# Two 64-token products on four 64x64 tiles, and a chunk's output projection half a slot behind its transposes

## The chip, the cores and the metric

The kernel runs on one core of a Trainium2 chip. The metric is the device time of one execution in microseconds; the time before is the median of three runs. The profile is of one further execution. Engines: PE is TensorE (matrix products; PEld are its weight loads), DVE is VectorE, ACT is ScalarE, POOL is GpSimd, and SP is SyncE, which here issues DMAs and nothing else. An engine's instructions run in the order of its own queue.

## The reference, cut to what matters

Two layers over 2 sequences of 1024 tokens with 256 features. The first adds a gated delta-rule attention and a mixture of low-rank experts to the input; the second adds a gated linear attention and a 2:4-sparse feed-forward unit. All numbers are float32. The change is in the first layer's attention only: 16 key heads and 32 value heads of 128 channels, two value heads to a key head.

```python
q, k, v = silu(causal_conv4(xn @ W_qkvz))       # q, k normalised per head, q * 128**-0.5
beta = sigmoid(b); g = -exp(A_log) * softplus(a + dt_bias)
def step(S, inp):                               # per sequence and head; S is 128 x 128
    qt, kt, vt, gt, bt = inp
    S = S * exp(gt)
    delta = (vt - kt @ S) * bt
    S = S + outer(kt, delta)
    return S, qt @ S
core = scan(step, 0, over the 1024 tokens)
gated = rmsnorm(core * silu(z)) * norm_w
out = gated @ W_out                             # (32*128) -> 256
```

## The kernel before

**Chunks.** The scan is computed in chunks of 64 tokens per sequence. A tile's 128 partitions hold 64 tokens of sequence 0 (partitions 0 to 63, `LO`) and the same 64 of sequence 1 (64 to 127, `HI`). Value heads go in 8 groups of four (`HPG`), which belong to two key heads (`KPG`); head n of a group belongs to key head m = n // 2. A group has 16 chunks; two neighbouring chunks are a pair, so there are 64 pairs and 128 chunks.

**One chunk.** With N the masked and decayed key products of a chunk, the update of a whole chunk needs the inverse of a 64x64 triangular matrix per sequence and head. The functions, in a pair's order:

- `pair_scores`: the decays `lb` are exponentiated (L508 to L512), q-k and k-k products are made (`kq`, L520), and DVE multiplies the two into `np` (L526): `np[:, 0]` is N, `np[:, 1]` the masked query products. SP then sends N to `nat` (four DMAs, L530) and to a DRAM buffer `natd` (two, L536), and brings its 8x8 diagonal blocks back as `n` (eight, L540).
- `pair_lanes`: DVE inverts the 8x8 blocks (L558 to L582); the result `E` goes through DRAM (L584, L586) into `U`.
- `pair_inverse`: PE and DVE join 8x8 inverses to 32x32 and 64x64 ones (`px`, `pyt`, `L`, `xs`). The result `invT` is 128x128 per head and chunk, block diagonal over the two sequences.
- `chunk_tokens`: keys and values are transposed to tokens on partitions; POOL scales the keys into `ktok` (L688), ACT the values into `vtok` (L697).
- `chunk_state`: PE makes `pks` and `pqs` from the state `S` (L716); DVE corrects `vtok` (L719), POOL decays `S` (L724); PE makes `pf` = inverse times values (L734), ACT copies it to `f` (L736); PE makes the state's increment `pS` from `ktok` and `f` (L743) and the output part `po` from `np[:, 1]` and `f` (L747); DVE adds `pS` to `S` (L754) and `po` to `qs` (L758) and gates with `z` (L760); ACT sums squares (L765).
- `chunk_output`: POOL makes the norm (L775 to L782); PE transposes (`yT`), ACT copies to `yTs` (L788), PE multiplies with `wo` (L792), DVE adds to the residual (L794).

`pf` multiplies whole 128x128 matrices, four per chunk. `pS` runs on four 64x64 tiles of the PE array (two row halves by two column halves), `po` on two (rows of a sequence to the same partitions of the output).

**Slots.** The layer runs in slots, one per pair. In a slot, generators of different pairs are interleaved step by step: each has a window of the slot (`add(kind, lo, hi, ...)`), and the one whose next step is due first goes. So a slot holds the scores of pair p, the inverse of pair p-1, the state of both chunks of pair p-2, the output of that pair's first chunk, and the output of pair p-3's second chunk, beside four blocks of the convolution (`conv_block`, L363) and two gates `z` for coming pairs. This gives the priority in which instructions are put on the engines' queues; an instruction whose inputs are expected later can be put behind others.

**PSUM.** All of PSUM is one pool of eight banks (`ps_tile`) for the whole program.

## Time and profile before

| What | us |
|---|---|
| median of three runs | 2953.18 |
| their range | 2949.0 to 2954.69 |
| profiled execution, its own time | 2948.61 |
| its span from first to last instruction | 2946.9 |
| PE busy in the span | 2647.8 |
| DVE, ACT, POOL busy | 1914.8, 1716.6, 1516.5 |
| granted PE clock, mean share | 0.971 |

How to read the lines that follow. The page gives each engine's busy time and its share of the span, then the span in 40 slices with the busy share in tenths. The chain of waits is followed back from the last instruction: at each step to what released it, or to the instruction before it on its engine. A line of the windows gives a stretch, its length and the busy time and instruction count of PE, PEld, DVE, ACT and POOL, then the granted clock, the DMA engines' busy share and GB/s. A line of waits names who waited for whom, the total, the count and the longest. A group has the line, engine, operation, output and inputs, shapes and count; then busy time, mean ns of one, and the engine's idle time before it with what ended it. A line of the chain in order of time has the start, the length, and the engine with what it writes and its line, or a DMA.

### The profile page before, as it was taken

How to read it: one execution, taken by the hardware profiler on the slowest of the kernel's cores; microseconds unless marked ns; L12 is line 12 of the kernel's file. 1: busy time of each engine (PE TensorE's matmuls, PEld its weight loads, DVE VectorE, ACT ScalarE, POOL GpSimd, SP SyncE). 2: the span in 40 equal slices, each digit the busy share in tenths (PEclk: the TensorE clock that was granted, in tenths of full speed). 3: DMA queues.
4: the chain of work that ended last, by engine and by line, in shares of the span. 5: the costliest groups of instructions: out<-in, count | busy, mean ns of one | idle time of the engine just before them, and what ended most of it. 6: DMA issues, size and time to landing. Idle time of an engine off the chain costs nothing.

```text
span 2946.9 us, 87779 instructions
## 1 busy us (share of the span) xinstructions
PE 2647.8 (90%) x36502; PEld 1680.6 (57%) x36502; DVE 1914.8 (65%) x3845; ACT 1716.6 (58%) x4121; POOL 1516.5 (51%) x2690
## 2 busy tenths in 40 slices
PE   6998689998999899989999999999989998989997
PEld 2444356665666566655655666566655665654565
DVE  7652666676677666767767666677676677645544
ACT  4432566675666666666666667666666666544321
POOL 2222456666666666666666666666665666630000
PEclk9998899999999999999999999999999999999999
DMA  3001111111111111111111111111111111110000
GB/s 77 4 1 57 37 28 35 36 43 28 35 35 43 28 35 35 44 28 43 34 38 28 42 35 35 28 42 36 36 27 35 28 37 20 29 57 3 1 15 15
DMA packets 265965, 95.22 MB, mean 32 GB/s; under 512 B 220512, under 2 KB 244192, under 8 KB 265568
## 3 DMA queue, kind: packets, MB, share of 16 engines
q1 hardware_dynamic: 261872, 86.67, 13.2%
q8 instruction: 287, 4.70, 0.7%
q10 hardware_dynamic: 3696, 2.95, 0.4%
q14 instruction: 110, 0.90, 0.1%
HBM read 53.63 MB, written 27.53 MB: 28 GB/s over the span
## 4 chain that ended last, share of the span: by engine, by line
PE 32%; DVE 22%; ACT 13%; POOL 12%; issue 7%; DMA 7%; SPq 6%; DVEq 0%; POOLq 0%; ACTq 0%
DVE conv L363 6%; PE pj L152 5%; SPq L540 3%; PE out L792 3%; ACT gsq L765 3%; DMA n<-natd 3%; DVE qs L758 2%; DMA natd<-np 2%; DVE S L754 2%; POOL S L724 2%; DVE z L760 2%; PE y L1074 2%; POOL rn L447 2%; PE pg L152 2%; SPq L530 2%
## 5 line engine op out<-in xcount | busy, mean ns | idle before, releaser
L363 DVE SCALAR_TENSOR_TENSOR conv<-raw,convw,conv 128x512 f32<-128x512 f32 x768 | 644.3, 841 | 188.6 <-ACT conv L358 184.2
L152 PE MATMUL pj<-xnT,w 128*128 128x512 f32 x1024 | 509.4, 622 | 8.5 <-DMA w<-in_W_qkvz 8.5
L792 PE MATMUL out<-wo,yTs 128*128 128x256 f32 x1024 | 284.1, 425 | 106.7 <-ACT yTs L788 106.7
L719 DVE SCALAR_TENSOR_TENSOR vtok<-pks,neG,vtok 128x128 f32<-128x128 f32 x480 | 144.8, 342 | 251.7 <-PE pks L716 247.4
L765 ACT ACTIVATE gsq<-z 128x128 f32<-128x128 f32 x512 | 157.7, 308 | 246.3 <-DVE z L760 240.9
L152 PEld LDWEIGHTS pj<-xnT,w 128*128 128x128 f32 x1024 | 188.8, 197 | 187.0 <-issue 182.1
L792 PEld LDWEIGHTS out<-wo,yTs 128*128 128x128 f32 x1024 | 200.6, 206 | 143.0 <-ACT yTs L788 113.4
L724 POOL TENSOR_TENSOR S<-S,eEnd 128x512 f32<-128x512 f32 x224 | 257.7, 1170 | 26.7 <-PE pqs L716 26.3
L152 PE MATMUL z<-wz,xnT 128*128 128x512 f32 x512 | 240.4, 593 | 0.0
L356 ACT COPY raw<-pj 128x512 f32<-128x512 f32 x256 | 147.5, 576 | 144.3 <-PE pj L152 95.5
L754 DVE TENSOR_TENSOR S<-S,pS 128x512 f32<-128x512 f32 x224 | 148.5, 684 | 123.8 <-POOL S L724 110.8
L734 PE MATMUL pf<-vtok,invT 128*128 128x128 f32 x1024 | 167.1, 289 | 31.4 <-DVE vtok L719 31.2
L347 POOL COPY raw<-tails 128x6 f32<-128x6 f32 x192 | 68.8, 359 | 239.4 <-DVE conv L363 189.7
L358 ACT ACTIVATE conv<-pj,convw 128x512 f32<-128x512 f32 x256 | 176.9, 691 | 0.0
L729 ACT ACTIVATE qs<-pqs,neG 128x128 f32<-128x128 f32 x480 | 136.3, 365 | 56.9 <-PE pqs L716 54.9
L372 ACT ACTIVATE kq<-conv 128x512 f32<-128x512 f32 x128 | 81.3, 635 | 144.3 <-DVE conv L363 141.4
L734 PEld LDWEIGHTS pf<-vtok,invT 128*128 128x128 f32 x1024 | 135.9, 190 | 50.8 <-DVE vtok L719 43.2
L782 POOL TENSOR_TENSOR z<-z,rms 128x512 f32<-128x512 f32 x128 | 145.5, 1136 | 10.1 <-POOL rms L779 0.2
L688 POOL TENSOR_TENSOR ktok<-kt,wend 128x512 f32<-128x512 f32 x120 | 145.6, 1213 | 7.5 <-ACT kt L684 7.5
L360 POOL COPY tails<-raw 128x6 f32<-128x6 f32 x192 | 60.7, 316 | 156.5 <-ACT raw L356 156.5
L743 PE MATMUL pS<-f,ktok 64*64 64x128 f32 x3840 | 132.5, 275 | 7.6 <-ACT f L736 7.5
L603 PE MATMUL px<-L,natm 32*32 32x32 f32 x8192 | 101.7, 198 | 40.8 <-DVE L L645 22.7
(323 smaller groups left out, 5885.0 us busy)
## 6 DMA issues: line engine op xcount, KB each, us to landing
lb<-grows SPq DMA_DIRECT2D x128, 128.0 KB
natd<-np SPq DMA_DIRECT2D x128, 128.0 KB
w<-in_W_qkvz SPq DMA_DIRECT2D x16, 512.0 KB
nat<-np SPq DMA_DIRECT2D x256, 32.0 KB
n<-natd SPq DMA_DIRECT2D x512, 4.0 KB
ed<-E SPq DMA_DIRECT2D x64, 128.0 KB
U<-ed SPq DMA_DIRECT2D x64, 128.0 KB
wz<-in_W_qkvz SPq DMA_DIRECT2D x16, 256.0 KB
```

The costliest lines, as they stand in the source:

```text
L152: k.nc.tensor.matmul(ps, lhsT_of(kt), rhs_of(kt), start=(kt == 0), stop=(kt == KT - 1))
L356: nc.scalar.copy(chunks(raw[:, :, KSIZE - 1 :]), pv)
L358: nc.scalar.activation(chunks(y), pv, AF.Copy, scale=tap(KSIZE - 1))
L363: k.anchor = nc.vector.scalar_tensor_tensor(y, shifted, tap(j), y, ALU.mult, ALU.add).ins
L688: nc.gpsimd.tensor_tensor(pair(x.k), bcast(kt, 2, 2), bcast(wend, 3, P), ALU.mult)
L719: nc.vector.scalar_tensor_tensor(x.v[:, i, :], pks[:, i, :], at(k.neG, i), x.v[:, i, :], ALU.mult, ALU.add)
L724: nc.gpsimd.tensor_tensor(k.S[:, b], k.S[:, b], bcast(k.eEnd[:, b, t, h.h0 : h.h0 + HPG], 2, P), ALU.mult)
L734: nc.tensor.matmul(pf[:, i, :], invT[:, i, :], x.v[:, i, :], start=True, stop=True)
L754: nc.vector.tensor_tensor(k.S[:, b], k.S[:, b], pS[b], ALU.add)
L765: nc.scalar.activation(sq, x.z[:, i, :], AF.Square, accum_out=x.sumsq[:, i : i + 1])
L782: nc.gpsimd.tensor_tensor(y, y, bcast(rms, 2, P), ALU.mult)
L792: nc.tensor.matmul(po[:, 0:D], yT[:, i, :], wo[:, i, :], start=(i == 0), stop=(i == HPG - 1))
```

## The change

In `chunk_state`, `pf` becomes eight 64x64 products per chunk. For the value heads of the first key head, a sequence's rows go to the same half of the output's partitions; for those of the second they go to the other half (`across`). So `pf` uses all four tiles, and f, the keys' `ktok`, the query products `np[:, 1]` and the state `S` hold the two sequences swapped for heads 2 and 3. `po` crosses back and also uses all four. The order of heads in both is 0, 2, 1, 3. Both products share a new PSUM tile `fo` of two banks, one per key head, in a pool of its own with one buffer; the shared pool keeps six banks in this layer.

To swap heads 2 and 3, DVE and POOL write that half to a side tile (`npo`, `ktoko`), and two DMAs on SP's queue move it across the partitions. `invT` is kept without its zero blocks. `eEnd`, the decay of a chunk, is swapped when it is made.

The last part of `chunk_output` becomes `chunk_project` and gets windows of its own: the first chunk's projection runs in the slot after its transposes, the second chunk's in the later half of the slot.

```diff
 def pair_scores(k, pools, pr):
-    for s in range(2):
-        by = kq[:, :, :, s].rearrange("p x m i -> p (x m) i")
-        nc.vector.tensor_tensor(pairs(pr.np[:, s]), pairs(lb), bcast(by, 2, 2), ALU.mult)
-        if s == 0:
-            yield
+    by = kq[:, :, :, 0].rearrange("p x m i -> p (x m) i")
+    nc.vector.tensor_tensor(pairs(pr.np[:, 0]), pairs(lb), bcast(by, 2, 2), ALU.mult)
+    yield
+    other = wk.tile([P, PC, 2, CT], F32, tag="npo", name=f"npo{pr.name}", bufs=1)
+    for m, out in enumerate((pr.np[:, 1, :, 0:2], other)):
+        two = slice(2 * m, 2 * m + 2)
+        nc.vector.tensor_tensor(out, lb[:, :, two], bcast(kq[:, :, m, 1], 2, 2), ALU.mult)
+    for rows, across in ((LO, HI), (HI, LO)):
+        nc.sync.dma_start(pr.np[across, 1, :, 2:4], other[rows])
     for n, r in enumerate(QUARTERS):
         nc.sync.dma_start(pr.nat[r], pr.np[r, 0, :, :, QUARTERS[n % 2]])
...
 def chunk_tokens(k, pools, x):
-        nc.gpsimd.tensor_tensor(pair(x.k), bcast(kt, 2, 2), bcast(wend, 3, P), ALU.mult)
+        other = wk.tile([P, 2, P], F32, tag="ktoko", name=f"ktoko{x.name}")
+        for m, out in ((1, other), (0, x.k[:, 0:2])):
+            wend = h.wend[:, c, 2 * m : 2 * m + 2]
+            nc.gpsimd.tensor_tensor(out, bcast(kt[:, m], 1, 2), bcast(wend, 2, P), ALU.mult)
+        for rows, across in ((LO, HI), (HI, LO)):
+            nc.sync.dma_start(x.k[across, 2:4], other[rows])
...
 def chunk_state(k, pools, x):
-                    nc.tensor.matmul(out[rows, two, :], q, k.S[:, b, two, :], start=True, stop=True)
+                    nc.tensor.matmul(out[rows, two, :], q, k.S[:, b ^ m, two, :], start=True, stop=True)
...
-    pf = four(k, f"pf{x.name}")
-    for i in range(HPG):
-        nc.tensor.matmul(pf[:, i, :], invT[:, i, :], x.v[:, i, :], start=True, stop=True)
+    fo = k.psum2.tile([P, KPG, 2, 2, P], F32, tag="fo", name=f"fo{x.name}")
+    pf, po = fo[:, :, 0], fo[:, :, 1]
+    across = lambda r, m: halves[r ^ m][1]
+    for i in range(2):
+        for m in range(KPG):
+            for r, rows in halves:
+                n = 2 * m + i
+                nc.tensor.matmul(pf[across(r, m), m, i, :], invT[rows, n, :], x.v[rows, n, :], start=True, stop=True)
...
-    po = four(k, f"po{x.name}")
-    for i in range(HPG):
-        for b, rows in halves:
-            nc.tensor.matmul(po[rows, i, :], x.pair.np[rows, 1, x.at, i, :], f[rows, i, :], start=True, stop=True)
+    for i in range(2):
+        for m in range(KPG):
+            for r, rows in halves:
+                n = 2 * m + i
+                nc.tensor.matmul(
+                    po[across(r, m), m, i, :], x.pair.np[rows, 1, x.at, n, :], f[rows, n, :], start=True, stop=True
+                )
...
 def chunk_output(k, pools, x):
-    yT = pools.work.tile([P, HPG, P], F32, tag="yT", name=f"yTs{x.name}")
-    nc.scalar.copy(yT, pt)
+    x.yT = pools.work.tile([P, HPG, P], F32, tag="yT", name=f"yTs{x.name}")
+    nc.scalar.copy(x.yT, pt)
     yield
+
+def chunk_project(k, pools, x):
+    nc, sm, h, c = k.nc, pools.small, x.h, x.c
+    wo = group_weights(k, pools, "o", h.grp)
     po = ps_tile(k, f"out{x.name}")
...
 def delta_layer(k, I):
-                add("output1", 0.05, 0.5, chunk_output(k, pools, pair(p - 3).chunks[1]))
+                one, two = pair(p - 3).chunks
+                add("output1", 0.05, 0.5, chunk_output(k, pools, two))
+                add("project0", 0.05, 0.4, chunk_project(k, pools, one))
+                add("project1", 0.55, 0.9, chunk_project(k, pools, two), "output1")
...
 def two_layers(ctx, tc, I, out):
-        delta_layer(k, I)
+        early.close()
+        with psum("psum1", 6) as k.psum, psum("psum2", 1) as k.psum2:
+            delta_layer(k, I)
```

Outside the layer the program has its eight banks as before, in pools of their own.

More of the change, by code (lines that the diff above doesn't have):

```diff
@@ L249, in delta_gates @@
         nc.tensor.matmul(ps, k.ones[rows], flat(g)[rows], start=True, stop=True)
-        nc.scalar.activation(flat(k.eEnd[:, b]), ps, AF.Exp)
+        by_key = lambda a: a.rearrange("p (t g m j) -> p t g m j", t=NTILE, g=NGROUP, m=KPG)
+        for m in range(KPG):
+            mine = by_key(flat(k.eEnd[:, b ^ m]))[:, :, :, m]
+            nc.scalar.activation(mine, by_key(ps)[:, :, :, m], AF.Exp)
         yield
@@ L653, in pair_inverse @@
     for n, r in enumerate(QUARTERS):
-        (nc.gpsimd.tensor_copy, nc.scalar.copy)[n % 2](invT[r, :, r], U[r])
+        (nc.gpsimd.tensor_copy, nc.scalar.copy)[n % 2](invT[r, :, QUARTERS[n % 2]], U[r])
     yield
@@ L670, in pair_inverse @@
     for q, copy in ((0, nc.scalar.copy), (2, nc.vector.tensor_copy)):
-        copy(invT[QUARTERS[q], :, QUARTERS[q + 1]], pyt[QUARTERS[q]])
+        copy(invT[QUARTERS[q], :, QUARTERS[1]], pyt[QUARTERS[q]])
     yield
@@ L685, in chunk_tokens @@
         x.k = wk.tile([P, HPG, P], F32, tag="ktok", name=f"ktok{x.name}")
-        pair = lambda a: a.rearrange("p (m i) c -> p m i c", m=KPG)
-        wend = h.wend[:, c, :].rearrange("p (m i) -> p m i", m=KPG)
-        nc.gpsimd.tensor_tensor(pair(x.k), bcast(kt, 2, 2), bcast(wend, 3, P), ALU.mult)
+        other = wk.tile([P, 2, P], F32, tag="ktoko", name=f"ktoko{x.name}")
[4 more added lines that the diff above has]
+            nc.sync.dma_start(x.k[across, 2:4], other[rows])
         yield
@@ L730, in chunk_state @@
         yield
-    pf = four(k, f"pf{x.name}")
-    for i in range(HPG):
-        nc.tensor.matmul(pf[:, i, :], invT[:, i, :], x.v[:, i, :], start=True, stop=True)
+    fo = k.psum2.tile([P, KPG, 2, 2, P], F32, tag="fo", name=f"fo{x.name}")
[6 more added lines that the diff above has]
+                nc.tensor.matmul(pf[across(r, m), m, i, :], invT[rows, n, :], x.v[rows, n, :], start=True, stop=True)
     f = wk.tile([P, HPG, P], F32, tag="f", name=f"f{x.name}")
-    nc.scalar.copy(f, pf)
+    by_key = lambda a: a.rearrange("p (m i) d -> p m (i d)", m=KPG)
+    flat = lambda a: a.rearrange("p m i d -> p m (i d)")
+    nc.scalar.copy(by_key(f), flat(pf))
     yield
     if not x.last:
-        pS = [four(k, f"pS{x.name}_{b}") for b in range(NB)]
+        pS = [four(k, f"pS{x.name}_{r}") for r in range(NB)]
         for i in range(HPG):
-            for b, rows in halves:
+            for r, rows in halves:
                 for cols in (LO, HI):
-                    nc.tensor.matmul(pS[b][cols, i, :], x.k[rows, i, cols], f[rows, i, :], start=True, stop=True)
-    po = four(k, f"po{x.name}")
-    for i in range(HPG):
-        for b, rows in halves:
-            nc.tensor.matmul(po[rows, i, :], x.pair.np[rows, 1, x.at, i, :], f[rows, i, :], start=True, stop=True)
+                    nc.tensor.matmul(pS[r][cols, i, :], x.k[rows, i, cols], f[rows, i, :], start=True, stop=True)
+    for i in range(2):
+        for m in range(KPG):
+            for r, rows in halves:
+                n = 2 * m + i
+                nc.tensor.matmul(
+                    po[across(r, m), m, i, :], x.pair.np[rows, 1, x.at, n, :], f[rows, n, :], start=True, stop=True
+                )
     yield
@@ L755, in chunk_state @@
     yield
-    no = po
+    no = flat(po)
     if not x.first:
-        nc.vector.tensor_tensor(qs, qs, po, ALU.add)
-        no = qs
-    nc.vector.tensor_tensor(x.z, no, x.z, ALU.mult)
+        nc.vector.tensor_tensor(by_key(qs), by_key(qs), no, ALU.add)
+        no = by_key(qs)
+    nc.vector.tensor_tensor(by_key(x.z), no, by_key(x.z), ALU.mult)
     yield
@@ L771, in chunk_output @@
     nc, sm, h, c = k.nc, pools.small, x.h, x.c
-    wo = group_weights(k, pools, "o", h.grp)
+    group_weights(k, pools, "o", h.grp)
     pair = lambda a: a.rearrange("p (m i) -> p m i", m=KPG)
@@ L786, in chunk_output @@
         nc.tensor.transpose(pt[:, i, :], y[:, i, :], k.ident)
-    yT = pools.work.tile([P, HPG, P], F32, tag="yT", name=f"yTs{x.name}")
-    nc.scalar.copy(yT, pt)
+    x.yT = pools.work.tile([P, HPG, P], F32, tag="yT", name=f"yTs{x.name}")
+    nc.scalar.copy(x.yT, pt)
     yield
+def chunk_project(k, pools, x):
+    nc, sm, h, c = k.nc, pools.small, x.h, x.c
+    wo = group_weights(k, pools, "o", h.grp)
     po = ps_tile(k, f"out{x.name}")
     for i in range(HPG):
-        nc.tensor.matmul(po[:, 0:D], yT[:, i, :], wo[:, i, :], start=(i == 0), stop=(i == HPG - 1))
+        nc.tensor.matmul(po[:, 0:D], x.yT[:, i, :], wo[:, i, :], start=(i == 0), stop=(i == HPG - 1))
     res = k.res[:, h.t0 + c, :]
@@ L849, in delta_layer @@
         k.tails = const.tile([P, 4 * KPG, NB, KSIZE - 1], F32, tag="tails", name="tails")
-        k.invT = [const.tile([P, PC, HPG, P], F32, tag=f"invT{i}", name=f"invT{i}") for i in range(2)]
+        k.invT = [const.tile([P, PC, HPG, CT], F32, tag=f"invT{i}", name=f"invT{i}") for i in range(2)]
         k.S = const.tile([P, NB, HPG, P], F32, tag="S", name="S")
@@ L1353, in two_layers @@
     k.keep = ctx.enter_context(tc.tile_pool(name="keep", bufs=1))
-    k.psum = ctx.enter_context(tc.tile_pool(name="psum", bufs=8, space=bass.MemoryType.PSUM))
+    psum = lambda name, bufs: tc.tile_pool(name=name, bufs=bufs, space=bass.MemoryType.PSUM)
     k.res = k.keep.tile([P, NTILE, D], F32, tag="res", name="res")
@@ L1364, in two_layers @@
     k.xnT = k.keep.tile([P, KT, N], F32, tag="xnT", name="xnT")
+    early = ctx.enter_context(ExitStack())
+    k.psum = early.enter_context(psum("psum0", 8))
     with tc.tile_pool(name="ln0", bufs=2) as pool:
@@ L1381, in two_layers @@
         expert_layer(k, I)
-        delta_layer(k, I)
+        early.close()
+        with psum("psum1", 6) as k.psum, psum("psum2", 1) as k.psum2:
+            delta_layer(k, I)
     with ExitStack() as scope:
         pool = lambda name, bufs: scope.enter_context(tc.tile_pool(name=name, bufs=bufs))
+        k.psum = scope.enter_context(psum("psum3", 8))
         pools = Pools()
```

## The prediction

> **What bounds the kernel now.** I read the page first: engine totals, the 40 slices and the chain of waits.

> ```profile
> PE 2647.8 (90%) x36502; PEld 1680.6 (57%) x36502; DVE 1914.8 (65%) x3845; ACT 1716.6 (58%) x4121; POOL 1516.5 (51%) x2690
> PE   6998689998999899989999999999989998989997
> PE 32%; DVE 22%; ACT 13%; POOL 12%; issue 7%; DMA 7%; SPq 6%; DVEq 0%; POOLq 0%; ACTq 0%
> ```

> The two disagree. TensorE (PE) is busy nine tenths of the time, but the chain that ended last spends a third of its time there. So I read the windows next. The delta layer runs in 64 slots from about 300 us; its steady part is the line of 372 to 2567 us.

> ```profile
> 372.00:2567.00 2195.00, 2009.31 (x32646) 1320.62 (x32644) 1522.21 (x3063) 1430.45 (x3569) 1373.57 (x2463) 0.98 0.16 34
> ```

> PE works 2009 of 2195 us there, VectorE (DVE) 1522, ScalarE (ACT) 1430, GpSimd (POOL) 1374: PE idles only 186 us. The waits of PE in that window say for whom:

> ```profile
> PE out L792 <- ACT yTs L788: 104.1, 52, 3.4
> PE pf L734 <- DVE vtok L719: 31.2, 47, 1.5
> PE pyt L669 <- DVE xs L663: 20.9, 15, 2.5
> PE px L603 <- DVE L L645: 17.4, 16, 3.3
> ```

> More than half of the idle time is the output projection standing right behind its own transposes. Then the groups, for the products that change:

> ```profile
> L734 PE MATMUL pf<-vtok,invT 128*128 128x128 f32 x1024 | 167.1, 289 | 31.4 <-DVE vtok L719 31.2
> L747 PE MATMUL po<-f,np 64*64 64x128 f32 x2048 | 135.1, 269 | 0.7 <-ACT f L736 0.7
> L743 PE MATMUL pS<-f,ktok 64*64 64x128 f32 x3840 | 132.5, 275 | 7.6 <-ACT f L736 7.5
> ```

> A float32 product is two matmul instructions. pS already runs four 64x64 tiles at once: 132.5/3840 = 34.5 ns per instruction. po, on two tiles, costs 66 ns, pf on the whole array 163 ns. Last, the chain in order of time, in one slot:

> ```profile
> 1379.92 1.21 DVE np L526 x2
> 1381.12 0.07 SPq L530
> ...
> 1383.90 2.36 DMA natd<-np
> ...
> 1390.40 1.70 DMA n<-natd
> ...
> 1392.94 0.57 DVE X L558
> ```

> This is the second bound. np goes out through four nat and two natd issues on SyncE's queue (SP), returns through eight n issues, and only then DVE's small inverses (L558) start: 12 to 13 us. Counting over the chain in the steady part, it passes here in 28 slots, for some 365 us (np 35, SP's issues 170, transfers 160). PE is the fullest engine, but a serial stretch of SP and DMA sets the end about as often.

> **The change, part by part.**

> *pf and po on four tiles.* pf becomes 8 products of 64x64 per chunk, 16 instructions, 2048 in all; at pS's 34.5 ns that is 70.7 us against 167.1: -96.4. po keeps its 2048 instructions, at 34.5 instead of 66 ns: 70.7 against 135.1: -64.4. Together -160.8 us of PE work.

> [...] In po now both row halves write one PSUM bank, and 8 products take 135.1/128 = 1.06 us, 132 ns each; a product that streams the same 128 columns through the whole array takes 326, so two overlap in one bank. [...]

> I go by the row. If only two of the four tiles run together, pf costs 2048 x 66 = 135 us (saving 32) and po nothing less.

> *A new wait in pf.* pf took heads 0, 1, 2, 3 as DVE scaled them; now it takes 0, 2, 1, 3. Head 2 comes two DVE steps of 342 ns after head 0 (the row of vtok L719), with pf standing before whatever PE has next, and f, pS and S behind it. In the 47 chunks where pf waits already I add 0.68 us: +32. Ends: 0 (scaling long done) and 128 x 0.68 = +88.

> *Output projection half a slot later.* The matmuls are the same 284 us; the 104.1 us of waiting go, as yTs is many us old by then. PE then meets its next input sooner: DVE's xs, L and vtok (31.2, 20.9, 17.4 us of waits today) are next late. I take half: -52, ends 0 and -104. In the last slots two projections pile up: +2.

> *The swap of half of np through SP.* Two mults of 128x256 replace one of 128x512 (rows 412 and 681 ns): +0.14 us x 64 = 9 us of DVE, of which its share of the chain, a quarter, counts: +2. Two issues enter SP's queue among nat, natd and n. A nat issue takes 0.62 us (2.66 us for four), so n lands 2 x 0.62 = 1.25 us later, with L558 behind it and, in DVE's order, the convolution taps, the S update, xs and z. Ends: 28 slots x 1.25 = +35; or 64 slots x 3.3 = +211, if nat also waits for both mults (0.82) and the 128 KB of the swap delay natd by half of its own 2.36 us (256 KB). I take 64 x 1.25 = +80: a shorter slot leaves L558 no spare time. The swapped np is read by po two slots later: hidden.

> *The swap of half of ktok.* Two POOL mults of 128x256 (751 ns, the row of natm) replace one of 1213: +0.29 x 120 = 35 us of POOL, at its share of the chain (16%) +6; ends 0 and 35. The 240 issues fall where SP idles: the ktok mult ends at 1378.9 and nat starts at 1380.5; the other ends at 1393.5, between n and the E transfer at 1396.1. pS reads ktok some 16 us after each; issue and landing take 3.6 us by natd's lines. If that cover failed, PE would wait at pS, up to 1 to 2 us per chunk.

> *At nothing, with what hides it.* Shared PSUM falls from 8 banks to 6 plus 2 for fo. Laying the tiles' first matmul to last read over time, without pf and po over five banks are in use 0.1% of the steady part; uncovered, PE would wait for a copy, 0.6 us. fo is single: the next pf comes 5.7 us or more after z has read po (1400.7 and 1406.4); uncovered, it costs that difference. The pool change at the layer's start hides behind the 8.5 us that PE waits for the first weights (L152). invT's copies keep their counts; two more eEnd activations come once.

> **Sum.** -160.8 + 32 - 52 + 2 + 2 + 80 + 6 = -91 us. The profiled execution took 2948.6 us (span 2946.9), 4.6 below the median of the three runs, 2953.2; I set the difference against the median: 2862 us, -3.1%. Its own range, with the ends of the n delay and of the projection's wait: 2800 to 2920.

> **Rivals.**

> *A. The chain decides, not PE's load: small gain.* If the order stays, only what lies on the chain counts. In the steady part it holds 39.5 us of pf, 8.7 of po, 81.3 of out and 10.6 of yTs. That saves 39.5 x 0.58 + 8.7 x 0.48 = 27, and 92 of the projection, of which PE's share of the chain (19%) of 284, 55 us, comes back at its new place: 64 in all. Against it 35 for nat and 8 for the mults: -21, so 2932. For it: PE's third of the chain. Against: PE's 92%; less load on the fullest engine moves all queues up.

> *B. Slower: the trip of np through SP becomes the pace of every slot.* Place: between np and L558. Price: up to 3.3 us x 64 = 211, against the 64 that rival A saves: +147, 3100. It decides once n lands over 64/64 = 1.0 us later in every slot and nothing else is slower than this loop. For it: 28 slots run so today, and L558 waits for n in another part. Against: DVE idles 31% of the steady part, so much of a late n is absorbed.

> [...]

> *D. All of it:* PE loses 160.8 and the full 104, n costs 35: -230, 2723.

> **How the numbers follow.** Forecast 0.45, A 0.20, B 0.17, C 0.10, D 0.08. About 0.2% (6 us) is what a measurement can tell from no change. Faster: the forecast's case, 0.43, most of A, 0.16, and D, 0.08: 0.67. Same: edges of A and the forecast: 0.05. Slower: B, C and a rest of A: 0.28. The range runs from 2780, leaving out D, to 2990, which takes in C and the milder half of B.

> **What would show it.** [...] The wait of out for yTs gone; waits of pf for vtok up by some 30 us. PE's busy time near 2487. The time from np to the landing of n up by about 1.25 us; if by 3, and the waits of L558 grow to a microsecond or more per slot, B. A slot on average 1.4 us shorter. I am wrong if PE's work falls by 160 us and its idle time rises by as much: then order and latencies, not load, set the pace.

## The result, and the profile after

The change makes the kernel slower: 2986.98 us (median of 4 runs, 2970.13 to 2992.39) against 2951.09 for the kernel before on the same chip, a ratio of 1.0114 with a 95% interval of 1.0078 to 1.0151. The forecast was 2862. The profiled execution took 2988.01 us. One execution of all those below, the profiled one of e13, took 6440 us; its trace is not used.

The page of after, in the same four places as before: engine totals, PE's slices, the granted clock in tenths, the chain.

```profile
PE 2649.8 (89%) x37526; PEld 1589.4 (53%) x37526; DVE 1886.8 (63%) x3909; ACT 1713.9 (57%) x4123; POOL 1552.4 (52%) x2810
PE   6998689888999899989998989899888988979998
PEclk9998899999999999999999999999999999989999
PE 42%; DVE 18%; ACT 12%; POOL 10%; issue 7%; SPq 6%; DMA 5%; DVEq 0%; ACTq 0%; POOLq 0%
```

PE is busy 2649.8 us, as before (2647.8), not the 2487 of the forecast. Yet the two products did shrink. The groups of after, by line:

```profile
L152 PE MATMUL pj<-xnT,w 128*128 128x512 f32 x1024 | 580.0, 696 | 8.5 <-DMA w<-in_W_qkvz 8.5
L756 PE MATMUL fo<-vtok,invT 64*64 64x128 f32 x2048 | 101.6, 285 | 13.3 <-DVE vtok L735 11.7 <-POOL S L740 0.9 <-POOL nb L478 0.4
L772 PE MATMUL fo<-f,np 64*64 64x128 f32 x2048 | 80.3, 272 | 0.7 <-ACT f L760 0.7
```

L756 is pf, L772 po: 181.9 us together, 120.3 less than before (302.2). But pj, the convolution's input product, which the change does not touch, grew by 70.6 us. Before it was:

```profile
L152 PE MATMUL pj<-xnT,w 128*128 128x512 f32 x1024 | 509.4, 622 | 8.5 <-DMA w<-in_W_qkvz 8.5
```

The same 1024 instructions with the same operands take 696 instead of 622 ns on average. The reason is in the clock: where the clock is granted in full, one of them takes 606 ns in after and 604 in before; where it is granted at half, 1096 ns in after, and 159 of them lie wholly there, 24 in before. The line of the steady part (granted clock third from the end; 0.98 before):

```profile
372.00:2567.00 2195.00, 1974.84 (x33006) 1210.46 (x33004) 1467.32 (x3059) 1407.00 (x3509) 1389.28 (x2543) 0.94 0.20 44
```

```profile
1498.97:1502.38 3.41, 3.41 (x52) 2.14 (x44) 3.38 (x7) 2.54 (x3) 2.92 (x7) 1.00 0.01 2
1502.38:1505.80 3.42, 1.72 (x69) 1.06 (x68) 2.55 (x7) 3.04 (x11) 1.96 (x6) 1.00 0.08 14
1505.80:1509.21 3.41, 3.10 (x67) 2.04 (x68) 1.55 (x3) 1.53 (x3) 2.84 (x8) 0.50 0.34 67
1509.21:1512.62 3.41, 3.41 (x57) 1.67 (x58) 1.44 (x4) 1.75 (x5) 2.41 (x5) 1.00 0.63 154
```

In the second, PE is busy for 1.72 of 3.42 us, because it waits for L in front of px. In the third it has work again, but at half rate: there px takes 1.08 us and the four pj instructions behind it 3.00, where the four at 1500.78 us took 1.98. The fourth is at full rate. In the steady part of after 56 full-rate windows are followed by a drop to half rate, and in 50 of them the longest wait of PE is this one, of px for L. Last, the waits of PE in the steady part, where out's 104.1 us were the largest before:

```profile
PE px L611 <- DVE L L653: 137.9, 58, 3.4
PE fo L756 <- DVE vtok L735: 11.7, 22, 1.1
```

The wait of out for yTs is gone (1.4 us in the whole span); that of px for L took its place (17.4 before). That of pf for vtok fell from 31.2.

**One sum for all kernels.** I counted over 60 slots of each trace: the slot's length is PE's idle time plus its busy time, and of the busy time each half-rate window is counted as losing half its 3.413 us. What is left is PE's work at full clock. (PE is busy for 95% of the half-rate windows in before and 92% in after, and pj takes 1096 ns there against 606, 1.81 times as long, so the loss is counted a little too high.)

| per slot, us | slot | = work at full clock | + lost at half rate (windows in 60 slots) | + idle |
|---|---|---|---|---|
| before | 36.38 | 32.56 | 0.74 (26) | 3.08 |
| after | 36.99 | 31.12 | 2.13 (75) | 3.74 |

So the change took 1.44 us of work from a slot, 86 us over 60, and got back 1.39 us of half-rate loss and 0.66 us of idling. DVE, ACT and POOL are busy for nearly the same time per slot in both (24.8, 23.7, 23.4 us in after; 25.2, 23.7, 22.8 before).

**Where n became late.** From the end of np's first mult, SP's first n issue comes after 9.10 us (before 6.03), the last ends after 13.23 (before 10.50): means over 59 slots. DVE waits for n in front of its small inverses; the steady part of before, then of after:

```profile
DVE X L558 <- DMA n<-natd: 9.8, 18, 1.7
```

```profile
DVE X L566 <- DMA n<-natd: 57.3, 37, 5.7
```

The first L of a pair (L639, before L631) starts 25.09 us after np's mult (23.74). But the L in front of which px waits (L653) is a later one: it is ready 40.7 us after np's mult, before 40.8, so the late n does not show in it. It is made from pyt, which PE itself has just finished: from pyt's end to this L's end 3.0 us pass on DVE, where a convolution tap stands between the two steps in 51 of 59 slots. In before that is 3.6 us, but there the output product stood on PE's queue in the meantime, and px waited only 17.4 us in all. No run put L ahead of the tap.

SP's queue in one slot of after (start, length, line, what is issued):

```profile
1503.02 0.66 SPq L538 DMA_DIRECT2D nat<-np  x1
1503.77 2.19 SPq L536 DMA_DIRECT2D np<-npo  x2
1506.01 1.96 SPq L538 DMA_DIRECT2D nat<-np  x3
1508.01 1.25 SPq L544 DMA_DIRECT2D natd<-np  x2
1509.37 1.18 SPq L604 DMA_DIRECT2D lb<-grows  x2
1511.10 4.15 SPq L548 DMA_DIRECT2D n<-natd  x8
```

The swap of np stands between the first nat and the other three in every slot. Here its two issues hold the queue for 2.19 us; on average 1.51 us pass between the first nat issue and the second, before 0.06. In 52 of 59 slots two ktok issues stand right ahead of the first nat, and where they wait for POOL, nat starts late: 1.07 us after np on average, before 0.03, and more than 0.5 us in 26 slots.

### The profile page after: what moved, and what is told of

Its sections match the earlier page's. It is cut to its first block, busy times and chain, and to the rows that moved or that the text cites. A ratio compares the mean times of both kernels' runs of the same rounds, so it can differ in the third digit from the quotient of the medians.

```text
span 2986.2 us, 90715 instructions
## 1 busy us (share of the span) xinstructions
PE 2649.8 (89%) x37526; PEld 1589.4 (53%) x37526; DVE 1886.8 (63%) x3909; ACT 1713.9 (57%) x4123; POOL 1552.4 (52%) x2810
## 4 chain that ended last, share of the span: by engine, by line
PE 42%; DVE 18%; ACT 12%; POOL 10%; issue 7%; SPq 6%; DMA 5%; DVEq 0%; ACTq 0%; POOLq 0%
PE pj L152 8%; DVE conv L366 5%; PE out L825 5%; DVE S L781 3%; ACT gsq L792 3%; SPq L548 3%; POOL S L740 2%; PE pks L732 2%; DMA natd<-np 2%; PE px L611 2%; DVE qs L785 2%; PE z L152 2%; PE y L1110 2%; SPq L538 2%; PE pqs L732 2%
## 5 line engine op out<-in xcount | busy, mean ns | idle before, releaser
L152 PE MATMUL pj<-xnT,w 128*128 128x512 f32 x1024 | 580.0, 696 | 8.5 <-DMA w<-in_W_qkvz 8.5
L152 PEld LDWEIGHTS pj<-xnT,w 128*128 128x128 f32 x1024 | 206.0, 215 | 211.3 <-issue 203.9
L792 ACT ACTIVATE gsq<-z 128x128 f32<-128x128 f32 x512 | 156.4, 306 | 186.2 <-DVE z L787 178.2
L825 PE MATMUL out<-wo,yTs 128*128 128x256 f32 x1024 | 260.2, 398 | 1.4 <-ACT yTs L815 1.4
L611 PE MATMUL px<-L,natm 32*32 32x32 f32 x8192 | 107.1, 205 | 172.1 <-DVE L L653 147.0
L152 PE MATMUL z<-wz,xnT 128*128 128x512 f32 x512 | 251.3, 614 | 0.0
L825 PEld LDWEIGHTS out<-wo,yTs 128*128 128x128 f32 x1024 | 187.1, 192 | 37.0 <-issue 11.3
L611 PEld LDWEIGHTS px<-L,natm 32*32 32x32 f32 x8192 | 93.7, 117 | 197.2 <-issue 172.0
L450 POOL TENSOR_TENSOR rms<-ms,mhalf 128x4 f32<-128x4 f32 x128 | 152.7, 1193 | 10.0
L732 PE MATMUL pks<-S,kq 128*64 128x256 f32 x960 | 146.8, 429 | 3.0 <-DVE S L781 2.9
L732 PEld LDWEIGHTS pks<-S,kq 128*64 128x64 f32 x960 | 65.8, 155 | 139.3 <-issue 111.6
L732 PE MATMUL pqs<-S,kq 128*64 128x256 f32 x960 | 126.3, 383 | 8.7 <-ACT z L417 8.7
```

What stands on the lines that cost most here:

```text
L152: k.nc.tensor.matmul(ps, lhsT_of(kt), rhs_of(kt), start=(kt == 0), stop=(kt == KT - 1))
L450: nc.gpsimd.tensor_tensor(out, x, k.mhalf[:, 0 : x.shape[1]], ALU.pow)
L611: k.nc.tensor.matmul(out[r, i, :], lhsT[r, i, :], rhs[r, i, :], start=True, stop=True)
L732: nc.tensor.matmul(out[rows, two, :], q, k.S[:, b ^ m, two, :], start=True, stop=True)
L792: nc.scalar.activation(sq, x.z[:, i, :], AF.Square, accum_out=x.sumsq[:, i : i + 1])
L825: nc.tensor.matmul(po[:, 0:D], x.yT[:, i, :], wo[:, i, :], start=(i == 0), stop=(i == HPG - 1))
```

## The experiments

Times are medians; ratios are to the kernel before, run beside each, with their 95% interval. Before itself lay between 2947 and 2959 us, so kernels are compared by ratio, a difference of 0.001 being 3 us. A difference of two ratios is known to 7 to 9 us, one with after to some 12. Slots, windows and waits come from the one profiled execution; against its kernel's median that was 9 us shorter in e9, 28 shorter in e10 and 9 longer in e18. The diffs show the lines that carry an edit, not all of it.

### Which part costs

**The tiles without the moved projection** (e1): after, with `chunk_project` put back into `chunk_output`.

```diff
-                add("project0", 0.05, 0.4, chunk_project(k, pools, one))
-                add("project1", 0.55, 0.9, chunk_project(k, pools, two), "output1")
```

> Four tiles and the swaps as in the changed kernel, but the output projection stays right behind its transposes. Theory U (uncovered): the moved projection left px alone with its wait for DVE's L (147 us in all), and the emptier 3.4 us stretches cost half-clock windows (74 against 25). Without the move the wait of px is small (under 40 us), the wait of out for yTs is back at about 100 us, half-clock windows fall to about 25 to 40, and the time is 2850 to 2920 us, below the kernel before. Theory Q (queue): the swap DMAs ahead of nat and n make every slot late; the time stays at 2960 to 3010 as in the changed kernel, with DVE's wait for n still near 67 us. Theory T (tiles): the four-tile products save little, the time is 2945 to 2990.

3022.35 us, 1.0242 [1.0223, 1.0262]: above the ranges of all three theories, with 80 half-rate windows and a slot of 37.65 = 31.19 + 2.28 + 4.18.

**The moved projection alone** (e2): before, with `chunk_project` and its two windows.

```diff
+                add("project0", 0.05, 0.4, chunk_project(k, pools, one))
+                add("project1", 0.55, 0.9, chunk_project(k, pools, two), "output1")
```

> The kernel before with only the output projection moved half a slot; pf and po as before, no swaps. Theory U: the wait of px for L goes up to 100 to 150 us, half-clock windows to 50 or more, time 2960 to 3050, no faster than before. Theory Q: the wait of out is gone, nothing is added to SP's queue, time 2850 to 2920, faster than before.

2926.64 us, 0.9925 [0.9905, 0.9944]: a gain of 22 us. It is faster, as theory Q had it, but the wait of px grows as theory U had it. Its slot is 35.92 = 32.41 + 0.57 (20 windows) + 2.94. The wait moved here as well, to px:

```profile
PE px L603 <- DVE L L645: 113.0, 61, 3.9
```

**The tiles without the swaps** (e7): e1 with np and ktok written in one go, as before, and no DMAs for them.

```diff
-    for rows, across in ((LO, HI), (HI, LO)):
-        nc.sync.dma_start(pr.np[across, 1, :, 2:4], other[rows])
```

> The tiles-only kernel (projection in its old place) without the swaps: np and ktok are made in one piece, no side tiles and no swap DMAs, so the swap of heads 2 and 3 is left out of the computation; products, PSUM and order of heads as in the change. Theory Q: all of the loss is gone, 2860 to 2930, faster than before, since PE's work falls by about 1.4 us a slot. Theory W: the work becomes idle time and half-clock windows (60 or more), 2940 to 3000. Theory P: 2980 to 3020.

3015.82 us, 1.0228 [1.0207, 1.0250]. So with the projection in its old place the small products themselves go with nearly all of the loss; the swaps' 4 us (1.0242 against 1.0228) are within the noise. The time lies in theory P's range, but the next run speaks against its cause. The slot is 37.50 = 31.15 + 2.25 (79 windows) + 4.10: the work fell by 1.4 us as it should, and 2.5 us of idling and half rate came in its place. The wait that grew is the old one, of out:

```profile
PE out L812 <- ACT yTs L808: 161.4, 51, 4.6
```

**Six and two PSUM banks alone** (e6): before, with pf and po in `fo`.

```diff
-    pf = four(k, f"pf{x.name}")
+    fo = k.psum2.tile([P, KPG, 2, 2, P], F32, tag="fo", name=f"fo{x.name}")
```

> The kernel before with only the PSUM of the change: six shared banks, and pf and po in the two-bank tile fo; their products as before, no swaps, projection in its old place. Theory Q (the swap DMAs on SP's queue make the slots late): no change, within 0.5% of before, as PSUM held over five banks 0.1% of the time. Theory P (PSUM: fewer banks make PE wait): 2980 or more, most of the 72 us that the tiles-only kernel lost. Theory W (less PE work only becomes idle time and half clock): no change.

2942.32 us, 0.9977 [0.9963, 0.9992]: with the products of before, the banks cost nothing.

### Where the swaps stand, and where the projection

**Swaps in later steps** (e3): np's swap behind the n issues, ktok's in steps of their own.

```diff
+                add("swap0", 0.9, 1.1, swap_keys(k, pair(p - 1).chunks[0]), "tokens0")
+                add("swap1", 0.5, 0.52, swap_keys(k, two), "tokens1")
```

> The changed kernel with the swap DMAs of np issued after the eight n issues and those of ktok in steps of their own in the middle and at the end of a slot. Theory U: np to the last n issue goes back from 12.5 to about 10 us, but px still waits for L over 100 us and half-clock windows stay above 50; time 2960 to 2990. Theory Q: time falls by 40 to 120 us, to 2870 to 2950.

3040.92 us, 1.0300 [1.0277, 1.0323]. This misfired: ktok's issues still stood right ahead of nat in 52 of 59 slots, and waited there for POOL longer; nat started 3.8 us after np's mult, not 1.07, and more than 0.5 us after it in 51 slots, not 26. It shows the price of a wait at the head of SP's queue, not that of late swaps.

**Swaps bound behind the last n** (e9): the same, but each swap tied to follow the slot's last n issue.

```diff
+    with k.tc.issue_after(k.last_n):
+        for rows, across in ((LO, HI), (HI, LO)):
+            nc.sync.dma_start(pr.np[across, 1, :, 2:4], other[rows])
```

> The changed kernel with all swap DMAs (np's and both chunks' ktok's) forced on SP's queue behind the slot's last n issue and ahead of the E transfer. Theory Q: np to the last n issue falls back to 10 to 10.5 us, DVE's wait for n to under 20 us, the time to 2860 to 2930, faster than the kernel before. Theory W: n is early again, but the time stays above 2960, with 60 or more half-clock windows.

2952.21 us, 1.0009 [0.9991, 1.0026]: the swaps' place in the queue was worth 31 us (1.0114 against 1.0009). nat again starts 0.03 us after np, the last n issue ends after 10.83 us, and the slot is 36.34 = 31.28 + 1.34 (47 windows) + 3.72. So n is early as theory Q had it, and the time is still not below before. The wait of px for L is no smaller than in after (147.5 us in the steady part, 137.9 in after). Against e2, which lacks the tiles and the swaps, e9 is 25 us slower (1.0009 against 0.9925).

**The projection in the gap before px** (e4): a later window for the first chunk's projection.

```diff
-                add("project0", 0.05, 0.4, chunk_project(k, pools, one))
+                add("project0", 0.25, 0.65, chunk_project(k, pools, one))
```

> The changed kernel with one number changed: the first chunk's projection has the window 0.25 to 0.65 of a slot in place of 0.05 to 0.4, which puts its matmuls between the second chunk's transposes and px on PE's queue. Theory U: the wait of px for L falls from 147 to under 40 us, half-clock windows to 30 or fewer, time 2800 to 2900, faster than both kernels. Theory Q: no change beyond 0.5%, 2970 to 3000.

3012.82 us, 1.0213 [1.0193, 1.0233]. px waits 84.1 instead of 147.0 us and the windows fall to 61, but the waits of yT and pS grow and idling goes to 4.60 us a slot. Both theories fell: covering px's wait with work that is needed elsewhere only moved the wait.

### The order on ScalarE

In e7 and after, f's copy in a pair's second chunk stands on ACT's queue behind two copies to invT; in before it stands first. It starts 1.3 to 1.4 us after pf's last product there, before 0.04. In the first chunk it starts 1.27 us late in after, behind other copies and scalings, 0.39 in e7 and 0.08 in before.

**f first, in after with late swaps** (e10).

```diff
+    k.last_f = nc.scalar.copy(by_key(f), flat(pf)).ins
+        with k.tc.issue_after(k.last_f):
             nc.scalar.activation(x.v[:, two, :], pv[:, two, :], AF.Copy, scale=h.norm[:, c, m : m + 1])
```

> The changed kernel with the swaps' transfers behind the slot's last n transfer, and with ScalarE's copy of f ahead of its copies invT<-U and vtok<-pv, as it stands in the kernel before. Theory Q (the small products let the planner put f's copy behind those copies; f comes 1.3 us after its products instead of 0.04 us, twice per slot, and everything behind f comes later): about 2952 - 60 x 1 = 2890 to 2925 us, f within 0.2 us of its products. Theory H (the half-rate windows of TensorE are what the tiles cost; the order on ScalarE hides beside other waits): 2945 to 2960 us, with some 47 half-rate windows as without the reordering.

2952.52 us, 0.9994 [0.9973, 1.0014], although f now starts after 0.05 us in the second chunk. In the first it stays at 0.94 us, as in e9, so this tests the second chunk alone. Its 12 runs spread from 2924.4 to 2958.8, and with them the clock: 0.966 in the shortest, 0.949 to 0.954 in those above 2950, some 20 us per 0.01.

**f first, tiles alone** (e11): the same edit in e7.

> The four tiles alone, projection in its old place, without the swaps (this leaves the swap of heads 2 and 3 between the row halves out, so their values are not the reference's), and with f's copy first on ScalarE. Without the reordering this kernel took 3015.8 us, 70 over before. Theory Q: at least half of the 70 us returns, 2930 to 2980 us. Theory H: 3005 to 3025 us, no change, with some 79 half-rate windows in 60 slots.

3008.50 us, 1.0204 [1.0191, 1.0217], 76 windows: theory Q fell in both. The 7 us against e7 are within the noise.

### The half-rate windows

**Two products in the gap of after** (e8).

```diff
         if s == 4:
+            fill = ps_tile(k, f"fill{pr.name}")
+            for kt in range(KT):
+                nc.tensor.matmul(fill, k.ident, k.xnT[:, kt, 0:512], start=(kt == 0), stop=(kt == KT - 1))
```

> The changed kernel with one more 128x128x512 product per slot ahead of the second px, on PE's queue between the transposes and px where PE waits 2.3 us for DVE's L; its result is never read. It adds 64 x 1.9 = 120 us of PE work. Theory W: the wait at px falls under 60 us, half-clock windows from 74 to 30 or fewer, and the time falls or stays, 2920 to 2985. If the half clock costs nothing on the path: 3000 to 3100.

2999.91 us, 1.0183 [1.0161, 1.0204]. The windows fell from 75 to 24 and the wait for L to 43.6 us; the slot is 37.23 = 33.22 + 0.68 + 3.32. 2.1 us of added work a slot cost 0.24 us. The clock came back and the time did not: theory W was right on the clock, not on the time.

**One product in front of each out, tiles alone** (e12): e7 with 128x128 by 256 columns behind each yT.

```diff
+    with k.tc.issue_after(last.ins):
+        nc.tensor.matmul(fill[:, 0:D], k.ident, k.xnT[:, 0, 0:D], start=True, stop=True)
```

> The four tiles alone, projection in its old place, without the swaps (again the swap of heads 2 and 3 is left out), and with one added product of 128x128 by 256 columns, whose result nobody reads, between each chunk's yT transposes and its output product, where TensorE waits 161 us in all for ScalarE's copy. Theory H: the product lies in that wait and so costs nothing, it keeps its window over half busy, the half-rate windows fall from 79 towards 30, and the time from 3015.8 to 2950 to 2985 us. Theory Q: windows may fall, but the time stays at 3005 us or more, as the order on ScalarE stays.

3057.07 us, 1.0375 [1.0361, 1.0388], 68 windows: this misfired. In the queue the product stood ahead of the pyt products of the inverse, and it left the gap mostly open: out's wait for yTs is 171.6 us.

**The gap in front of the slot's first out, tiles alone** (e13, two products of 512 columns behind pyt; e16, one).

```diff
+    if x.at == 1:
+        with k.tc.issue_after(k.last_pyt):
+            nc.tensor.matmul(fill, k.ident, k.xnT[:, 0, 0:512], start=True, stop=True)
```

> The four tiles alone, projection in its old place, without the swaps (the swap of heads 2 and 3 is left out), as in the run that took 3015.8 us, and with two added products of 128x128 by 512 columns (0.94 us each, nobody reads them) once per slot, behind the pyt products and in front of the slot's first output product, where TensorE idles for 2.3 us and the output product then runs at half rate (3.60 instead of 1.99 us). Theory H (half-rate windows are the price of the gap): the fill lies in the gap, the output product runs in 2.0 us, the windows fall from 79 to 30 or fewer in 60 slots, and the time to 2925 to 2965 us. Theory L (another chain, of DVE, ScalarE and POOL, is as long as the slot whatever the clock does): windows fall, but the time stays at 2990 to 3030 us.

> The four tiles alone, projection in its old place, without the swaps (the swap of heads 2 and 3 is left out), with one product of 128x128 by 512 columns (0.94 us) per slot in front of the slot's first output product; with two it took 3000.7 us at a clock of 0.967, without any 3015.8 at 0.940. Theory H: the two products were too many, PE's work was the limit, and one gives 2940 to 2985 us. Theory L (the slot hangs on the way from z over yT's copy to the output product, which the order with the projection behind the transposes puts in front of px): 2990 to 3010 us, the half-rate windows fewer than 79, and the wait out<-yT of 161 us little smaller than without.

e13 took 3000.74 us, 1.0171 [1.0157, 1.0184], at a clock of 0.967 to 0.969. e16 took 2996.39, 1.0149 [1.0131, 1.0167], with 39 windows; out's wait for yTs was still 110.9 us. So in this order filling the gap brings 17 to 23 of the 67 us: the times are theory L's. Most of the clock is back, and 44 to 50 us of the loss stay.

**One product in the gap before px** (e18: after; e17: after with late swaps, e9; e14: e10; e15: e2).

```diff
         if s == 4:
+            fill = ps_tile(k, f"fill{pr.name}")
+            nc.tensor.matmul(fill, k.ident, k.xnT[:, 0, 0:512], start=True, stop=True)
```

> The changed kernel, swaps where it has them, with one product of 128x128 by 512 columns (0.94 us, nobody reads it) per slot in front of the second px, where TensorE waits 147 us in all. If the half-rate windows and the late n are two separate prices, the fill brings the same 42 us as with late swaps: 2935 to 2955 us. If the late n alone holds the slot here, 2980 to 3000 us at a clock of 0.96 or more: the clock then comes back, and TensorE only waits longer for L.

> The changed kernel with the swaps behind the last n and one product of 0.94 us in front of the second px, f's copy where the planner puts it. With f first it took 2911.2 us at a clock of 0.977. If the order on ScalarE has no part in it, 2905 to 2920 us; if it has, 2930 us or more, with more than 25 half-rate windows.

> The changed kernel with late swaps and f first on ScalarE (median 2952.5, its runs 2924 to 2959 with clocks from 0.966 down to 0.949), and with one added product of 128x128 by 512 columns (0.94 us, nobody reads it) once per slot in front of the second px, where TensorE waits 150 us in all. Theory H: half-rate windows fall under 30, the clock is 0.965 or more in every run, and the time is 2905 to 2930 us. Theory L: clock up, time 2945 to 2960 us as without it.

> Before with the projection alone moved (2926.6 us, clock 0.974, 20 half-rate windows that cost 0.57 us a slot), and with the same one product in front of the second px, where TensorE waits 113 us in all. Theory H: the windows fall under 12 and the time to 2900 to 2920 us. Theory L: 2922 to 2940 us.

| | swaps early | swaps behind n |
|---|---|---|
| no fill | after: 2986.98, 1.0114 | e9: 2952.21, 1.0009 |
| one product | e18: 2979.44, 1.0066 [1.0045, 1.0086] | e17: 2910.36, 0.9853 [0.9835, 0.9871] |

e14 took 2911.18, 0.9864 [0.9847, 0.9880], as e17 does; so the order on ScalarE in the second chunk has no part in it. e15, the moved projection with the fill but without tiles, took 2922.81, 0.9917 [0.9903, 0.9932]: there the fill brings nothing that can be measured (0.9925 without it). e17, after with late swaps and one product that computes nothing of use, is with e14 the fastest kernel of the study, 43 us faster than before. Of these the moved projection alone gives 22 (e2); the tiles, once n is early and the gap filled, give 19 (e17 against e15), where they cost 25 without the fill.

The two do not simply add: alone the fill brings 14 us and the late swaps 31, each known to 12, together they bring 77. Each price hides the other. In e18's profiled execution, its longest, the windows fall from 75 to 35 and the slot stays at 36.98 us. What grew is the wait for n (waits of DVE in the steady part of e18; 57.3 us in after):

```profile
DVE X L566 <- DMA n<-natd: 114.7, 47, 6.9
DVE X L566 <- DMA ktok<-ktoko: 27.4, 5, 6.9
```

On PE the wait of px for L falls from 137.9 to 78.9 us, and others grow by about as much, those of yT, pqs, pS and pyt, and of px for ACT. With n late, the time that full clock saves is waited away. In e17 n is early: SP's queue in one slot has the swaps last,

```profile
1524.95 2.65 SPq L536 DMA_DIRECT2D nat<-np  x4
1527.65 1.25 SPq L542 DMA_DIRECT2D natd<-np  x2
1528.99 1.18 SPq L606 DMA_DIRECT2D lb<-grows  x2
1530.71 4.34 SPq L546 DMA_DIRECT2D n<-natd  x8
1535.14 1.35 SPq L550 DMA_DIRECT2D np<-npo  x2
1536.59 1.19 SPq L721 DMA_DIRECT2D ktok<-ktoko  x2
```

DVE waits for n 8.5 us in all at L575, and the clock is at 0.99:

```profile
372.00:2567.00 2195.00, 2011.41 (x34491) 1239.20 (x34494) 1594.31 (x3165) 1438.43 (x3619) 1447.45 (x2621) 0.99 0.20 45
```

Its slot is 35.75 = 32.44 + 0.26 (9 windows) + 3.06: against e9 it has 1.16 us more work, 1.08 us less half-rate loss and 0.66 us less idling.

## Why the prediction was wrong

**pf and po, -160.8 us.** The step that failed. As a size it was too big: 120.3 us in the groups. A burst of 16 instructions takes 0.62 us (po, 39 ns each), pS's 32 take 1.10 (34.5 each), so a part of a burst seems not to shrink with its length. pf's bursts take 0.67 us in the median but 0.79 on average, though 127 of 128 lie in full-rate windows; only 8 have a wait inside, and what lengthens the others is open. But the error that decides is another: all of it was counted as time because PE is busy nine tenths. The work left PE (1.44 us a slot at full clock) and came back as half rate and idling. In time, from kernel to kernel: the moved projection gave 22 us (e2), the tiles with late swaps then cost 25 (e9), and the swaps' place in the queue 31 (after); that makes the 34 us of loss. The prediction's own last sentence named this as the way to be wrong, without half rate. That 2987 still lies inside its range, by 3 us, is mostly luck: the end of 2990 takes in the milder half of B and a rival C (chance 0.10), in which only two of the four tiles run at once, so that PE saves 32 us and the time is 2991. No run shows the limit that C assumes: both row halves write a bank of fo, and po runs at 39 ns, not 66.

**Half rate: not in the sum at all.** The 0.971 of the clock stood in the table. Read in windows of 3.413 us it says that 25 windows of the steady part run at half rate, 43 us, and that each of the 21 drops to it follows a window in which PE was busy under half. Work taken from PE in the stretch around a wait left more such windows: 74 in after, 126 us, so 83 us went there. The window before a drop need not be idle: 1.72 us of work in 3.42 did not prevent the drop.

**The new order of pf's heads, +32.** Not seen: pf waits 11.7 us in after, less than the 31.2 of before; with early n it waits 26.5 (e9), as without tiles (25.6, e2).

**The projection, -52.** Right in direction, less than half in size: alone it gains 22 us (e2). That PE "meets its next input sooner" was right, but what is next late is px alone, in nearly every slot (58 times 2.4 us), and behind it comes a half-rate window.

**np's swap through SP, +80 from 1.25 us.** The mechanism was right, the delay too small and its price too high: the last n issue comes 2.7 us later. The swap's own two issues make 1.45 us of this, near the forecast. What was missed are ktok's issues, booked at nothing "where SP idles": they wait at the head of the queue for POOL (873.9 us at L700 in all), and nat behind them starts 1.07 us late on average. The price is 31 us with half rate as it is (after against e9), 63 once it is gone (e18 against e17). That is rival B's place and its condition (n more than 1.0 us late), well under its price of up to 211. Rival A had the right idea of the sum, that only what lies on the chain counts, but no cost that could turn it into a loss.

**PSUM at nothing.** Right with the products of before: e6 does not lose. In after PE waits 8.7 us at pqs for ACT's z and 4.7 us at yT for DVE's S, neither of which these products read (e18: 18.8 and 19.6; e2, with eight banks: no such row). That points to PSUM banks, but no run shows it.

**What stays open.** Why the tiles alone, with the projection in its old place, lose 67 us (e7). Filling the gap brings back 17 to 23 of it, and the order on ACT in the second chunk at most some 7. Out's wait for yTs grew by 57 us in the steady part, and filling the gap takes most of that away without the time; which chain then holds the slot was not settled. That the place of the swaps and the clock together make after's loss is shown by e9 and e17; why the tiles are then worth 19 us, with 120 us less of PE work, is not. That an idle stretch as such lowers the clock rests on the windows of the traces, not on a run that changed nothing else.

## What to carry to other kernels

Work taken from the fullest engine is time only if nothing else sets the pace; ask per slot which wait ends last, and count a saving in front of that wait as idling (here 1.44 us of work left a slot, and the slot grew from 36.38 to 36.99 us). Read the mean granted clock as a number of half-rate windows (0.94 in after: 74), look where they lie, and ask whether an edit lengthens the idle stretch in front of them; a product without use, put into a wait, can pay for itself, but only where half-rate windows follow that wait in many slots and nothing else holds the slot (46 us from e9 to e17, 14 from after to e18, 2 from e2 to e15). A DMA that waited for its input at the head of SP's queue delayed the issues behind it (nat started 1.07 us after np on average in after, 3.8 in e3, 0.03 in before): place new issues behind the last urgent one by an explicit order, not by a due time.

## What was unexpected in the hardware

- Half a window of idling was nearly always followed by half rate: in the steady part of after, 52 of 56 drops come behind a full-rate window in which PE was busy less than half, and no such window was followed by full rate (in before 21 were followed by a drop and 2 were not). Of the full-rate windows in the steady parts of before and after in which PE was busy for 0.5 to 0.65, 3 of 52 were followed by a drop, and of those in which it was busy for more, 1 of 1058. In after the drop lasts one window 38 times and two 18 times. In e17, 9 windows are left.
- In three runs the time of eight slots came out near a whole number of clock windows. In e7 eight slots in a row, the eight pairs of a head group, take 300.2 to 300.6 us six times running, which is 88 windows of 3.413 us (300.4); in e11 five of six groups take 300.2 to 300.4, and in e10 five of six 286.5 to 286.9, near 84 windows (286.7). In before and after no such step shows (288 to 292 and 293 to 299 us in six groups). That the clock's grid sets these times was not shown.
- An added product of some 1.0 us of PE work per slot, 66 us in all in e17's trace, made e9 46 us faster (1.0009 to 0.9853).
